# A product by a chosen matrix plus the input: two rows of a sample on each partition, and products in 64x64 tiles

## The chip, the core and the metric

The kernel runs on one core of a Trainium2 chip. The core has engines that run side by side and meet only through semaphores: TensorE (PE) multiplies matrices, VectorE (DVE) works on elements, ScalarE (ACT) only issues loads here, GpSimd (POOL) passes on semaphores and copies a little, and SyncE (SP) issues stores. Sixteen DMA engines move data between the memory of the chip and SBUF, the working memory with 128 partitions. Products land in PSUM, a second memory of 128 partitions.

The metric is the device time in microseconds. The kernel before takes 323.05 us, the median of 3 runs (322.87 to 323.2).

## The reference

```python
# x: (128, 128, 1024) float32; itok_B_0_7: (128,) int32, 0 to 7
# L0_cond_weights: (8, 128, 128) float32
w = weights[subjects]                       # one 128x128 matrix for each sample
out = jnp.einsum('bct,bcd->bdt', x, w)
return x + out
```

For each of 128 samples b, the output is x[b] plus the product of the transposed matrix of its subject with x[b]. A sample has 128 rows (c) of 1024 numbers (t), half a megabyte. 67.1 MB go in, as many come out, and the eight matrices are half a megabyte together.

## The kernel before

A sample lies in SBUF with one row c on each partition: 128 partitions of 1024 numbers. Four samples make a slot of 2 MB, and SBUF holds 12 slots (`x_all`, `SLOTS`). The program runs over 32 turns (`NT`) of four samples, in two halves of two samples (`H`, `G`).

- ScalarE issues 128 loads of one sample each (`load`, line 134), in order. From the thirteenth turn on it waits until the stores of the slot's previous turn have finished (`s_slot`).
- GpSimd waits for the loads of each turn and tells TensorE (`s_ready`).
- TensorE runs a loop of 32 turns (line 268). `multiply` (line 168) waits for the matrices (`s_go`) and for the input (`s_ready`), and makes four products for a half: two samples, and for each the two 512-wide halves of t. A product has the 128x128 matrix of its sample as the stationary operand and streams 512 columns. Its result takes one PSUM bank; the two halves of a turn use one half of PSUM each (`ps[0]`, `ps[1]`).
- VectorE runs a loop of 32 turns (line 263). `add` (line 183) waits for the products of a half, adds PSUM to the input in SBUF (128 x 2048 elements) and writes the sum over the input, in the same slot. `place` (line 163) then copies the two matrices of the next turn's half out of `w_all` into `w0` to `w3`, since the subject of a sample is known only at run time.
- SyncE waits for adds (`s_added`) and issues a store of 2 MB for each of the first 20 turns (`store`, line 142); in the middle of the program it lags four more turns behind the adds (`BEHIND`). The last 12 turns go out in six stores of 4 MB (`PAIR`).

Before the loops the matrices are brought in: one load of 512 KB with 4 KB on each partition, two transposes on VectorE (lines 208 and 227) and 16 copies (line 230, four of them on GpSimd) put row c of every matrix on partition c. Meanwhile TensorE runs three products of zeros (line 200, `IDLE`).

On the DRAM side a load is described as 32 pieces of 16 KB (`ROWS` = 4 rows each), and on the SBUF side as 128 pieces of 4 KB. A store reads 16 KB from each partition and writes it as four rows of 4 KB to four samples.

Of the kernel before, what the change touches and what calls it, by code (L numbers as in the profile page):

```python
# [25 lines left out]
F32 = mybir.dt.float32  # L26
I32 = mybir.dt.int32
ALU = mybir.AluOpType


G = 2
H = 2

N = 512

SLOTS = 12

P_SLOTS = 2

BEHIND = 4  # L40

EARLY = 8
LAST = 8

PAIR = 2
WHOLE = 6

DMA = 16

SORTED = 18  # L50

IDLE = 3

ROWS = 4

# [25 lines left out]
def kernel(  # L81
# [7 lines left out]
    nc = tc.nc  # L89
    B, C, T = x.shape  # L90
    S, _, D = weights.shape
    NT = B // (G * H)

    def sbuf(name, *shape, dtype=F32):
        return ctx.enter_context(nc.sbuf_tensor(name, list(shape), dtype)).ap()


    room = -(nc.sbuf_base + -nc.sbuf_base % 32) % ALIGN
    if room:
        sbuf("room", C, room // 4)  # L100
    x_all = sbuf("x_all", C, SLOTS * H * G * T)
    xs = [
        x_all[:, i * H * G * T : (i + 1) * H * G * T].rearrange("c (q t) -> c q t", t=T)
        for i in range(SLOTS)
    ]
    w_all = sbuf("w_all", C, S, D)
    w_raw, w_mid, w_late = (xs[SLOTS - 1][:, q, :] for q in range(3))
    ws = [sbuf(f"w{i}", C, 1, D) for i in range(H * G)]
    zeros = sbuf("zeros", C, N)
    given, near, wrap = (sbuf(name, 1, B, dtype=I32) for name in ("given", "near", "wrap"))  # L110
    index = sbuf("index", 1, B + H * G, dtype=I32)
    ps = [
        ctx.enter_context(nc.psum_tensor(f"ps{i}", [D, G, T], F32)).ap() for i in range(P_SLOTS)
    ]
# [4 lines left out]
    s_zeros = tc.alloc_semaphore("s_zeros")  # L119
    s_product = tc.alloc_semaphore("s_product")  # L120
# [5 lines left out]
    s_slot = [tc.alloc_semaphore(f"s_slot{k}") for k in range(SLOTS)]  # L126
    s_head = tc.alloc_semaphore("s_head")
    s_sort = tc.alloc_semaphore("s_sort")

    def emptied(i):  # L130
        turns = i // SLOTS
        return DMA * (H * G + 1) * turns - (DMA * G if i >= SLOTS and i % SLOTS == 0 else 0)

    def load(engine, i, q):
        transfer(
            nc,
            engine,
            xs[i % SLOTS][:, q, :],
            x[i * H * G + q].rearrange("(a r) t -> a (r t)", r=ROWS),
        ).then_inc(s_head if i * H * G + q < G else s_slot[i % SLOTS], DMA)  # L140

    def store(i, n):
        at = i % SLOTS * H * G * T
        return transfer(
            nc,
            nc.sync,
            out[i * H * G : (i + n) * H * G].rearrange("g d t -> d g t"),
            x_all[:, at : at + n * H * G * T].rearrange(
                "d (o t) -> d o t", o=1 if i >= NT - WHOLE else n
            ),  # L150
        )

    def subjects_of(i):
        _, subject = nc.values_load_multi_w_load_instructions(
            index[0:1, i] if isinstance(i, slice) else index[0:1, bass.ds(i * (H * G), H * G)],
            engines=[mybir.EngineType.DVE],
            min_val=0,
            max_val=S - 1,
            skip_runtime_bounds_check_because="the index is clamped on the chip above",
        )  # L160
        return subject

    def place(h, subject):
        for q in range(h * G, (h + 1) * G):
            copy = nc.vector.tensor_copy(ws[q], w_all[:, bass.ds(subject[q], 1), :])  # L165
        copy.then_inc(s_go, 1)

    def multiply(slot, h):
        nc.tensor.wait_ge(s_go, 1).then_inc(s_go, -1)
        nc.tensor.wait_ge(s_ready, 1).then_inc(s_ready, -1)  # L170
        for q in range(h * G, (h + 1) * G):
            for t in range(0, T, N):
                at = slot * (H * G * T) + (q * T + t)
                mm = nc.tensor.matmul(  # L174
                    ps[h][:, q % G, t : t + N],
                    ws[q][:, 0, :],
                    x_all[:, bass.ds(at, N)],
                    start=True,
                    stop=True,
                )  # L180
        mm.then_inc(s_product, 1)

    def add(slot, h):
        mine = x_all[:, bass.ds(slot * (H * G * T) + h * G * T, G * T)]
        nc.vector.wait_ge(s_product, 1).then_inc(s_product, -1)  # L185
        nc.vector.tensor_tensor(  # L186
            mine, ps[h].rearrange("d g t -> d (g t)"), mine, ALU.add
        ).then_inc(s_added, 1)

    with tc.tile_critical():  # L190

        nc.sync.dma_start(
            w_raw, weights.rearrange("s (u j) d -> (s u) (j d)", j=S)
        ).then_inc(s_wall, DMA)
        nc.sync.dma_start(given, subjects.rearrange("(o b) -> o b", o=1)).then_inc(s_given, DMA)

        nc.vector.memset(zeros, 0.0).then_inc(s_zeros, 1)  # L197
        nc.tensor.wait_ge(s_zeros, 1)
        for _ in range(IDLE):
            nc.tensor.matmul(  # L200
                ps[P_SLOTS - 1][:, G - 1, :N], zeros[:, :D], zeros, start=True, stop=True
            )

        nc.vector.wait_ge(s_wall, DMA)
        nc.vector.transpose(  # L208
            w_mid.rearrange("p (e h w j) -> p j h e w", e=S, h=4, w=4), w_raw
        ).then_inc(s_sort, 1)  # L210
        nc.vector.memset(index[:, B:], 0).then_inc(s_index, 1)  # L211
        nc.vector.wait_ge(s_given, DMA)
        nc.vector.tensor_scalar(near, given, -S, S - 1, ALU.max, ALU.min).then_inc(s_index, 1)  # L213
# [3 lines left out]
        nc.vector.tensor_tensor(index[:, :B], near, wrap, ALU.add).then_inc(s_index, 1)  # L217
        for i in range(NT):
            if i == SLOTS - 1:
                nc.scalar.wait_ge(s_sort, SORTED)  # L220
            if i >= SLOTS:
                nc.scalar.wait_ge(s_slot[i % SLOTS], emptied(i))
            for q in range(H * G):
                load(nc.scalar, i, q)

        nc.vector.wait_ge(s_sort, 1)
        nc.vector.transpose(w_late, w_mid).then_inc(s_sort, 1)  # L227

        def sort(engine, o, v):
            engine.tensor_copy(  # L230
                w_all[32 * v : 32 * (v + 1), 2 * o : 2 * (o + 1), :],
                w_late[32 * o : 32 * (o + 1)].rearrange("c (e v d) -> c v e d", v=4, d=D)[:, v],
            ).then_inc(s_sort, 1)

        nc.vector.wait_ge(s_sort, 2)
        nc.gpsimd.wait_ge(s_sort, 2)
        for o in range(4):
            for v in range(4):
                sort(nc.gpsimd if v == 3 else nc.vector, o, v)
        for i in range(NT):  # L240
            if i == 0:
                nc.gpsimd.wait_ge(s_head, DMA * G).then_inc(s_ready, 1)
                nc.gpsimd.wait_ge(s_slot[0], DMA * G).then_inc(s_ready, 1)
            else:
                nc.gpsimd.wait_ge(s_slot[i % SLOTS], emptied(i) + DMA * H * G).then_inc(s_ready, H)

        for i in [*range(NT - SLOTS), *range(NT - SLOTS, NT, PAIR)]:
            n = 1 if i < NT - SLOTS else PAIR
            nc.sync.wait_ge(s_added, (i + n + (BEHIND if EARLY <= i < NT - LAST else 0)) * H)
            if i == 0:  # L250
                nc.sync.dma_start(
                    out[: H * G].rearrange("g d t -> d g t"), xs[0]
                ).then_inc(s_slot[0], DMA)
            elif i + n < NT:
                store(i, n).then_inc(s_slot[i % SLOTS], DMA)


        nc.vector.wait_ge(s_index, 4)
        nc.vector.wait_ge(s_sort, SORTED)
        subject = subjects_of(slice(0, H * G))  # L260
        for h in range(H):
            place(h, subject)
        with nc.vector.Fori(0, NT) as turn:  # L263
            subject = subjects_of(turn + 1)
            for h in range(H):
                add(turn % SLOTS, h)
                place(h, subject)
        with nc.tensor.Fori(0, NT) as turn:
            for h in range(H):
                multiply(turn % SLOTS, h)  # L270

    with tc.tile_critical() as waits:
        for i in range(NT - SLOTS, NT - PAIR, PAIR):
            nc.scalar.wait_ge(s_slot[i % SLOTS], emptied(i + SLOTS))
    last = store(NT - PAIR, PAIR)

    tc.add_manual_dep(
        last.ins,
# [31 lines left out]
```

## Time and profile before

| | |
|---|---|
| median of 3 runs | 323.05 us |
| span of the profiled execution, first to last instruction | 320.9 us |
| TensorE busy | 248.9 us (78%), 518 records, mean granted clock 0.893 |
| VectorE busy | 172.6 us (54%) |
| DMA | 134.76 MB, 420 GB/s over the span |
| loads of x | 128 of 512 KB |
| stores | 20 of 2048 KB and 6 of 4096 KB |
| first product of a sample | 14.54 us |
| last add ends | 295.1 us |

How to read the rows: a group of instructions is given with line, engine, operation, output and inputs, the count behind the x, then busy time in us and mean ns of one, then the idle time just before them and what ended it. PE is the matmul records, PEld the weight loads. The rows of busy tenths and GB/s cut the span into 40 slices of 8 us; a 9 is a slice that is 90% busy or more. PEclk is the clock that TensorE was granted, in tenths of full speed. A row of a timeline has the start and the length in us first. A row of windows has the stretch, its length, then the busy time and number of records of PE, PEld, DVE and POOL, then the granted clock, the DMA share and GB/s.

### The profile page before, as it was taken

What the parts mean: (1) busy time and instruction counts of PE and PEld (TensorE: products, weight loads), DVE (VectorE), ACT (ScalarE), POOL (GpSimd) and SP (SyncE); (2) the same over time, 40 slices, a digit from 0 to 9 for tenths busy, and PEclk for the clock granted to TensorE, in tenths of its full rate; (3) what the DMA queues carried; (4) which work ended last, traced back from release to release, by engine and by line L of the source; (5) the groups of instructions that cost most, each with busy time, mean ns of one, the idle gap of its engine ahead of it and who ended that gap; (6) DMA issues with size and microseconds to landing.
All of it is one profiled execution on the core that took longest, in us unless ns stands there. A gap on an engine that the chain in (4) does not pass through costs nothing. (4 is left out here: it accounts for less than half of the span.)

```text
span 320.9 us, 2386 instructions
## 1 busy us (share of the span) xinstructions
PE 248.9 (78%) x518; PEld 102.8 (32%) x518; DVE 172.6 (54%) x216; POOL 1.9 (1%) x8
## 2 busy tenths in 40 slices
PE   6199999999997699998498469988599957874000
PEld 2134444444433244443133224333244422331000
DVE  4636776777676167775435362675367745066000
POOL 0200000000000000000000000000000000000000
PEclk9679999999999599999789797999799989599555
DMA  7999999999999999999999999999999999999996
GB/s 294 425 425 412 426 423 432 429 423 425 425 425 425 425 424 425 425 429 425 429 435 431 427 427 429 425 425 425 425 425 425 425 425 425 427 427 455 429 445 274
DMA packets 10803, 134.76 MB, mean 420 GB/s; under 512 B 2481, under 2 KB 2482, under 8 KB 3122
## 3 DMA queue, kind: packets, MB, share of 16 engines
q1 hardware_dynamic: 4658, 67.64, 49.7%
q10 hardware_dynamic: 6144, 67.12, 49.6%
q14 instruction: 1, 0.01, 0.0%
HBM read 67.63 MB, written 67.11 MB: 420 GB/s over the span
## 5 line engine op out<-in xcount | busy, mean ns | idle before, releaser
L174 PE MATMUL ps<-x_all,w 128*128 x512 | 243.8, 635 | 42.0 <-PEq L170 34.3
L186 DVE TENSOR_TENSOR x_all<-ps,x_all 128x2048 f32 x64 | 146.7, 2292 | 117.3 <-DVEq L185 117.3
L174 PEld LDWEIGHTS ps<-x_all,w 128*128 128x128 f32 x512 | 100.9, 203 | 185.2 <-issue 184.6
L165 DVE COPY w<-w_all 128x128 f32 x132 | 23.2, 219 | 0.8 <-DVE w_all L230 0.8
L200 PE MATMUL ps<-zeros 128*128 128x512 f32 x6 | 5.2, 1033 | 1.7 <-DVE zeros L197 1.7
L230 DVE COPY w_all<-x_all 32x256 f32<-32x256 f32 x12 | 3.9, 326 | 0.4
L208 DVE STREAM_TRANSPOSE x_all<-x_all 128x1024 f32<-128x1024 f32 x1 | 2.0, 1992 | 3.1 <-DMA x_all<-in_L_cond_weights_dram 3.1
L200 PEld LDWEIGHTS ps<-zeros 128*128 128x128 f32 x6 | 1.8, 328 | 3.7 <-issue 2.1
L230 POOL COPY w_all<-x_all 32x256 f32<-32x256 f32 x4 | 1.7, 425 | 8.3 <-DVE x_all L227 8.1
L227 DVE STREAM_TRANSPOSE x_all<-x_all 128x1024 f32<-128x1024 f32 x1 | 1.2, 1225 | 0.0
L197 DVE MEMSET zeros<- 128x512 f32 x1 | 0.5, 485 | 1.0 <-SPq L190 1.0
L217 DVE CUSTOM_DVE_ANT_0 index<-near,wrap 1x256 uint16<-1x256 uint16 x1 | 0.3, 280 | 0.0
L215 DVE TENSOR_SCALAR wrap<-near 1x128 int32<-1x128 int32 x1 | 0.2, 215 | 0.0
L213 DVE TENSOR_SCALAR near<-given 1x128 int32<-1x128 int32 x1 | 0.2, 205 | 0.0
L297 POOL MEMSET const-bfloat16-1.0<- 128x1 bf16 x1 | 0.1, 100 | 0.0
L297 POOL MEMSET const-float32-0.0<- 128x1 f32 x1 | 0.1, 98 | 0.2 <-issue 0.2
L297 POOL MEMSET const-uint8-127<- 128x1 uint8 x1 | 0.1, 98 | 0.0
L297 POOL MEMSET const-float32-1.0<- 128x1 f32 x1 | 0.1, 97 | 0.0
L297 DVE BASE_LOAD x1 | 0.0, 21 | 0.1
L211 DVE MEMSET index<- 1x4 int32 x1 | 0.1, 62 | 0.0
## 6 DMA issues: line engine op xcount, KB each, us to landing
x_all<-in_x_dram ACTq DMA_DIRECT2D x128, 512.0 KB, 34.2
out_dram<-x_all SPq DMA_DIRECT2D x20, 2048.0 KB, 18.3
out_dram<-x_all SPq DMA_DIRECT2D x6, 4096.0 KB, 30.3
x_all<-in_L_cond_weights_dram SPq DMA_DIRECT2D x1, 512.0 KB, 3.7
given<-in_itok_B_dram SPq DMA_DIRECT2D x1, 0.5 KB
```

What stands on the lines that cost most here:

```text
L165: copy = nc.vector.tensor_copy(ws[q], w_all[:, bass.ds(subject[q], 1), :])
L174: mm = nc.tensor.matmul(ps[h][:, q % G, t : t + N], ws[q][:, 0, :], x_all[:, bass.ds(at, N)], start=True, stop=True,)
L186: nc.vector.tensor_tensor(mine, ps[h].rearrange("d g t -> d (g t)"), mine, ALU.add).then_inc(s_added, 1)
L197: nc.vector.memset(zeros, 0.0).then_inc(s_zeros, 1)
L200: nc.tensor.matmul(ps[P_SLOTS - 1][:, G - 1, :N], zeros[:, :D], zeros, start=True, stop=True)
L208: nc.vector.transpose(w_mid.rearrange("p (e h w j) -> p j h e w", e=S, h=4, w=4), w_raw).then_inc(s_sort, 1)
L213: nc.vector.tensor_scalar(near, given, -S, S - 1, ALU.max, ALU.min).then_inc(s_index, 1)
L215: nc.vector.tensor_scalar(wrap, near, 0, S, ALU.is_lt, ALU.mult).then_inc(s_index, 1)
L217: nc.vector.tensor_tensor(index[:, :B], near, wrap, ALU.add).then_inc(s_index, 1)
L227: nc.vector.transpose(w_late, w_mid).then_inc(s_sort, 1)
L230: engine.tensor_copy(w_all[32 * v : 32 * (v + 1), 2 * o : 2 * (o + 1), :], w_late[32 * o : 32 * (o + 1)].rearrange("c (e v d) -> c v e d", ...
L297: nc = _bacc.Bacc("TRN2", target_bir_lowering=False, num_devices=1)
```

## The change

A sample now lies on 64 partitions with two neighbouring rows (`R` = 2) on each, 2048 numbers. Two samples (`H`) fill the 128 partitions, one in the lower half and one in the upper, and two such pairs (`P`) make a turn. Inputs have 8 places of one pair each, 1 MB (`x_in`, `IN`), and sums have 8 slots of one turn each, 2 MB (`x_out`, `OUT`). So a sum is no longer written over its input: an input place is free when its add has run, and a slot of sums is free when its store has finished (`s_out`, which GpSimd passes on to VectorE as `s_room`).

A row of the sample is c = 2a + r with a the partition and r the row on it, and likewise for the output row d = 2a + e. The product is therefore split into four 64x64 products: for each output row e, the sum over r = 0 and 1, accumulated in PSUM. `multiply` makes for each pair of samples 4 pieces (e, half of t) x 2 (r) x 2 (sample h) = 16 products. The innermost loop goes over the two samples, whose pieces are shifted by two so that they write to different banks. The loop of TensorE now covers eight pairs with fixed addresses and runs 8 times.

The matrices come with the rows of both parities on one partition (64 partitions, 8 subjects, pieces of 1 KB), and three copies (two on VectorE, one on GpSimd, `SHARE`) put the columns into the order (r, e, a) for the lower and the upper half of the partitions. There are no transposes. `place` copies a 64x256 matrix for each sample. Five products of zeros run at the start instead of three.

Loads are 64 of 1 MB (8 KB on each partition). Stores stay 20 of 2 MB and 6 of 4 MB, and each reads 16 or 32 KB from a partition and writes it in rows of 8 KB.

```diff
-G = 2
 H = 2
+P = 2
+R = 2
-SLOTS = 12
+IN = 8
+OUT = 8
-BEHIND = 4
+BEHIND = 3
-WHOLE = 6
+WHOLE = 12
-IDLE = 3
+IDLE = 5
+SHARE = 6
...
+    def load(j):
+        at = j % IN * SIZE
         transfer(
             nc,
-            engine,
-            xs[i % SLOTS][:, q, :],
-            x[i * H * G + q].rearrange("(a r) t -> a (r t)", r=ROWS),
+            nc.scalar,
+            x_in[:, at : at + SIZE],
+            x[j * H : (j + 1) * H].rearrange("h (b r) t -> (h b) (r t)", r=ROWS),
...
-            out[i * H * G : (i + n) * H * G].rearrange("g d t -> d g t"),
-            x_all[:, at : at + n * H * G * T].rearrange(
-                "d (o t) -> d o t", o=1 if i >= NT - WHOLE else n
-            ),
+            out[i * Q : (i + n) * Q].rearrange("(p h) (a r) t -> (h a) p (r t)", h=H, r=R),
+            x_out[:, at : at + n * P * SIZE].rearrange("d (o f) -> d o f", o=1),
...
-    def place(h, subject):
-        for q in range(h * G, (h + 1) * G):
-            copy = nc.vector.tensor_copy(ws[q], w_all[:, bass.ds(subject[q], 1), :])
+    def place(p, subject):
+        for h in range(H):
+            copy = nc.vector.tensor_copy(
+                ws[p][h * A : (h + 1) * A],
+                w_all[h * A : (h + 1) * A, bass.ds(subject[p * H + h], 1), :],
+            )
         copy.then_inc(s_go, 1)
-    def multiply(slot, h):
+    def multiply(k):
+        p = k % P
         nc.tensor.wait_ge(s_go, 1).then_inc(s_go, -1)
         nc.tensor.wait_ge(s_ready, 1).then_inc(s_ready, -1)
-        for q in range(h * G, (h + 1) * G):
-            for t in range(0, T, N):
-                at = slot * (H * G * T) + (q * T + t)
-                mm = nc.tensor.matmul(
-                    ps[h][:, q % G, t : t + N],
-                    ws[q][:, 0, :],
-                    x_all[:, bass.ds(at, N)],
-                    start=True,
-                    stop=True,
-                )
+        pieces = [(e, t) for e in range(R) for t in range(0, T, N)]
+        for b in range(len(pieces)):
+            for r in range(R):
+                for h in range(H):
+                    e, t = pieces[(b + 2 * h) % len(pieces)]
+                    rows = slice(h * A, (h + 1) * A)
+                    at = k * SIZE + r * T + t
+                    mm = nc.tensor.matmul(
+                        ps[p][rows, e, t : t + N],
+                        ws[p][rows, 0, r * D + e * A : r * D + (e + 1) * A],
+                        x_in[rows, at : at + N],
+                        start=r == 0,
+                        stop=r == R - 1,
+                    )
         mm.then_inc(s_product, 1)
...
         nc.vector.tensor_tensor(
-            mine, ps[h].rearrange("d g t -> d (g t)"), mine, ALU.add
+            x_out[:, bass.ds(turn % OUT * (P * SIZE) + p * SIZE, SIZE)],
+            ps[p].rearrange("d r t -> d (r t)"),
+            x_in[:, bass.ds(turn % (IN // P) * (P * SIZE) + p * SIZE, SIZE)],
+            ALU.add,
         ).then_inc(s_added, 1)
+    def sort(engine, h, first, last):
+        engine.tensor_copy(
+            w_all[h * A : (h + 1) * A, first:last].rearrange("c s (r e a) -> c (s r) e a", r=R, e=R),
+            w_raw[:, first * R * D : last * R * D].rearrange(
+                "c (g a e) -> c g e a", a=D // R, e=R
+            ),
+        ).then_inc(s_sort, 1)
...
+        for j in range(NP):
+            if j >= IN and j % P == 0:
+                nc.scalar.wait_ge(s_added, j - IN + P)
+            load(j)
...
+        sort(nc.vector, 0, 0, S)
+        sort(nc.vector, 1, SHARE, S)
+        nc.gpsimd.wait_ge(s_wall, DMA)
+        sort(nc.gpsimd, 1, 0, SHARE)
...
         with nc.vector.Fori(0, NT) as turn:
             subject = subjects_of(turn + 1)
-            for h in range(H):
-                add(turn % SLOTS, h)
-                place(h, subject)
-        with nc.tensor.Fori(0, NT) as turn:
-            for h in range(H):
-                multiply(turn % SLOTS, h)
+            nc.vector.wait_ge(s_room, 1).then_inc(s_room, -1)
+            for p in range(P):
+                add(turn, p)
+                place(p, subject)
+        with nc.tensor.Fori(0, NP // IN):
+            for k in range(IN):
+                multiply(k)
```

The order of the instructions on TensorE, from the products of zeros into the loop, before (ISA rows set an address, `ps0` is the first half of PSUM, `w0` the matrix of a sample):

```order
L200 MATMUL ps1<-zeros 128x512 [waits s_zeros]
L200 MATMUL ps1<-zeros 128x512 x2
L192 UNCONDITIONAL_BRANCH
L268 UNCONDITIONAL_BRANCH
L174 ISA [waits s_go,s_ready]
L174 MATMUL ps0<-x_all,w0 128x512
```

and now, where `w0` holds the matrices of both samples of a pair, one in each half of the partitions:

```order
L223 MATMUL ps1<-zeros 128x512 [waits s_zeros]
L223 MATMUL ps1<-zeros 128x512 x4
L214 UNCONDITIONAL_BRANCH
L272 UNCONDITIONAL_BRANCH
L186 MATMUL ps0<-x_in,w0 64x512 [waits s_go,s_ready]
L186 MATMUL ps0<-x_in,w0 64x512 x15
L186 MATMUL ps1<-x_in,w1 64x512 [waits s_go,s_ready]
L186 MATMUL ps1<-x_in,w1 64x512 x15
```

Two more products of zeros stand ahead of the loop, and 16 products of 64 rows stand between two waits where 4 of 128 rows with an address each stood.

On VectorE, from the landing of the matrices to the first index registers, before (`near`, `wrap` and `index` are the subjects, brought into range):

```order
L208 STREAM_TRANSPOSE x_all<-x_all 128x8x4x8x4 [waits s_wall]
L211 MEMSET index 1x4
L213 TENSOR_SCALAR near<-given 1x128 [waits s_given]
L215 TENSOR_SCALAR wrap<-near 1x128 [waits s_index]
L217 ISA index<-near,wrap 1x256 [waits s_index]
L227 STREAM_TRANSPOSE x_all<-x_all 128x1024 [waits s_sort]
L230 COPY w_all<-x_all 32x256 [waits s_sort]
L230 COPY w_all<-x_all 32x256 x11
L154 TENSOR_LOAD index [waits s_sort,s_index]
```

and now:

```order
L225 MEMSET index 1x4
L205 COPY w_all<-x_out 64x2048 [waits s_wall]
L205 COPY w_all<-x_out 64x512
L238 TENSOR_SCALAR near<-given 1x128 [waits s_given]
L240 TENSOR_SCALAR wrap<-near 1x128 [waits s_index]
L242 ISA index<-near,wrap 1x256 [waits s_index]
L158 TENSOR_LOAD index [waits s_sort,s_index]
```

Two transposes and twelve copies gave way to two longer copies, which now stand ahead of the index steps.

On ScalarE, the loads of x, before:

```order
L67 DMA x_all<-in_x_dram 128x1024 x44
L67 DMA x_all<-in_x_dram 128x1024 [waits s_sort]
L67 DMA x_all<-in_x_dram 128x1024 x3
L67 DMA x_all<-in_x_dram 128x1024 [waits s_slot0]
L67 DMA x_all<-in_x_dram 128x1024 x3
L67 DMA x_all<-in_x_dram 128x1024 [waits s_slot1]
```

and now, from the start of the program:

```order
L311 UNCONDITIONAL_BRANCH [waits barrier_Pool_Activation_PE_DVE_SP_release]
L311 UNCONDITIONAL_BRANCH [waits SP_sequencer_49]
L70 DMA x_in<-in_x_dram 128x2048 x8
L70 DMA x_in<-in_x_dram 128x2048 [waits s_added]
L70 DMA x_in<-in_x_dram 128x2048
```

The first wait for room stood after 48 loads of half a megabyte, and it stands now after 8 of one megabyte; it is a wait for adds and no longer for stores.

More of the change, by code (lines that the diff above doesn't have):

```diff
@@ L100 @@
         sbuf("room", C, room // 4)
[L101 to L108, printed above, removed]
-    zeros = sbuf("zeros", C, N)
[L110 to L114, printed above, removed]
+    x_in = sbuf("x_in", C, IN * SIZE)
+    x_out = sbuf("x_out", C, OUT * P * SIZE)
+    w_all = sbuf("w_all", C, S, R * D)
+    w_raw = x_out[:A, (OUT * P - 1) * SIZE :]
+    zeros = sbuf("zeros", C, N)
+    index = sbuf("index", 1, B + Q, dtype=I32)
+    ps = [ctx.enter_context(nc.psum_tensor(f"ps{p}", [C, R, T], F32)).ap() for p in range(P)]
     s_given = tc.alloc_semaphore("s_given")
@@ L217 @@
         nc.vector.tensor_tensor(index[:, :B], near, wrap, ALU.add).then_inc(s_index, 1)
+        nc.gpsimd.wait_ge(s_zeros, 1).then_inc(s_room, OUT)
         for i in range(NT):
[L219 to L240, printed above, removed]
+            if i - OUT in stored:
+                n = 1 if i - OUT < NT - WHOLE else PAIR
+                nc.gpsimd.wait_ge(s_out[i % OUT], stored[i - OUT]).then_inc(s_room, n)
@@ L241 @@
             if i == 0:
-                nc.gpsimd.wait_ge(s_head, DMA * G).then_inc(s_ready, 1)
-                nc.gpsimd.wait_ge(s_slot[0], DMA * G).then_inc(s_ready, 1)
-            else:
[L245 to L255, printed above, removed]
+                nc.gpsimd.wait_ge(s_head, DMA).then_inc(s_ready, 1)
@@ L272 @@
+        with nc.tensor.Fori(0, NP // IN):
+            for k in range(IN):
+                multiply(k)
     with tc.tile_critical() as waits:
[L273 to L275 removed]
+        for i, n in stores[:-1]:
+            if i >= NT - OUT:
+                nc.scalar.wait_ge(s_out[i % OUT], stored[i])
+    last = store(*stores[-1])
     tc.add_manual_dep(
```

63 lines of the change are left out of this document (37 added, 26 removed).

## The prediction

> **What bounds the kernel now.** I read the page's head first, then the table of DMA queues, then the groups of instructions.
>
> ```profile
> span 320.9 us, 2386 instructions
> ...
> PE 248.9 (78%) x518; PEld 102.8 (32%) x518; DVE 172.6 (54%) x216; POOL 1.9 (1%) x8
> ...
> PE   6199999999997699998498469988599957874000
> ...
> PEclk9679999999999599999789797999799989599555
> DMA  7999999999999999999999999999999999999996
> GB/s 294 425 425 412 426 423 432 429 423 425 425 425 425 425 424 425 425 429 425 429 435 431 427 427 429 425 425 425 425 425 425 425 425 425 427 427 455 429 445 274
> DMA packets 10803, 134.76 MB, mean 420 GB/s; under 512 B 2481, under 2 KB 2482, under 8 KB 3122
> ...
> q1 hardware_dynamic: 4658, 67.64, 49.7%
> q10 hardware_dynamic: 6144, 67.12, 49.6%
> ```
>
> The two queues together fill 49.7 + 49.6 = 99.3% of the sixteen DMA engines' span, and nearly every slice moves about 425 GB/s: 134.76 MB at 425 GB/s is 317.1 us of the 320.9. The transfers bound this kernel, and no idle time is left there to win. The span is 2.15 us short of the median of the three runs (323.05); I sum against the span and add those 2.15 us.
>
> TensorE is the second resource, and it is not far behind.
>
> ```profile
> L174 PE MATMUL ps<-x_all,w 128*128 x512 | 243.8, 635 | 42.0 <-PEq L170 34.3
> L186 DVE TENSOR_TENSOR x_all<-ps,x_all 128x2048 f32 x64 | 146.7, 2292 | 117.3 <-DVEq L185 117.3
> L174 PEld LDWEIGHTS ps<-x_all,w 128*128 128x128 f32 x512 | 100.9, 203 | 185.2 <-issue 184.6
> L165 DVE COPY w<-w_all 128x128 f32 x132 | 23.2, 219 | 0.8 <-DVE w_all L230 0.8
> ...
> L230 DVE COPY w_all<-x_all 32x256 f32<-32x256 f32 x12 | 3.9, 326 | 0.4
> ...
> L230 POOL COPY w_all<-x_all 32x256 f32<-32x256 f32 x4 | 1.7, 425 | 8.3 <-DVE x_all L227 8.1
> ```
>
> The code writes 256 products (128 samples, two halves of T), and the profile has 512 matmul records: each float32 product is two records, each with its own weight load. Their mean of 635 ns is no pace, because records overlap. The pace is read from the starts of the weight loads, one for each record, and from the adds:
>
> ```profile
> 2.68 0.34 PEld L200 LDWEIGHTS ps<-zeros 128*128 128x128 f32 x1 [0.52 <-issue]
> 3.53 0.34 PEld L200 LDWEIGHTS ps<-zeros 128*128 128x128 f32 x1 [0.52 <-issue]
> ...
> 60.15 0.19 PEld L174 LDWEIGHTS ps<-x_all,w 128*128 128x128 f32 x1 [0.24 <-issue]
> 60.58 0.19 PEld L174 LDWEIGHTS ps<-x_all,w 128*128 128x128 f32 x1 [0.24 <-issue]
> ```
>
> ```profile
> 59.94 2.29 DVE L186 TENSOR_TENSOR x_all<-ps,x_all 128x2048 f32 x1 [0.81 <-DVEq L185]
> ...
> 67.00 2.29 DVE L186 TENSOR_TENSOR x_all<-ps,x_all 128x2048 f32 x1 [0.81 <-DVEq L185]
> ```
>
> ```profile
> 31.00:100.00 69.00, 68.59 (x157) 28.77 (x156) 49.22 (x58) 0.00 (x0) 1.00 1.01 425
> ```
>
> A record takes 0.43 us at the full clock (60.15 to 60.58) and 0.85 us at the slow one (2.68 to 3.53). From 31 to 100 us TensorE never rests and the granted clock is 1.00. There four samples, which are 16 records, take 67.00 - 59.94 = 7.06 us: 16 x 0.429 = 6.86, and 0.2 for two hand-overs, or 0.1 for each pair of samples. In and out, four samples are 4.19 MB, which takes 9.87 us at 425 GB/s. So TensorE has 2.8 us in hand out of every 9.87. All 512 records at this pace are 220 us, and doubled they are 440 us: this margin does not survive a doubling.
>
> **The change, part by part.**
>
> *Products.* A sample is now 64 partitions with two rows in each, so it needs four 64x64 products (two row parities in, two out) for each half of T where one 128x128 product stood. For a pair of samples that is 16 products instead of 4, each still streaming 512 columns; with two records each that is 32 records for a pair, and 2048 in all. No row of before shows a product of 64x64. The bounds from the nearest row are these. A 64x64 product holds a quarter of the array; if four were always under way, a record would cost 0.429 / 4 = 0.107 us, and 2048 would cost 220 us as now. If each has the array to itself, a record costs 0.429 us and 2048 cost 879 us. I take the middle value, two at a time, 0.215 us for a record, because of the code: the innermost loop alternates between the two samples of a pair, one reading partitions 0 to 63 and writing 0 to 63, the other reading and writing 64 to 127. Those share neither rows nor columns. But all 8 products of one sample read the same half and write the same half, so they follow one another, and half of the array stays empty. That gives 1024 steps of 0.429 us = 439.3 us, and with 64 hand-overs of 0.1 us 445.7 us.
>
> [...]
>
> *Start.* Rows of before:
>
> ```profile
> 0.96 0.41 SPq L192 DMA_DIRECT2D x_all<-in_L_cond_weights_dram  x1
> ...
> 1.43 0.32 SPq L195 DMA_DIRECT2D given<-in_itok_B_dram  x1
> ```
>
> ```profile
> 1.67 5.16 PE L200 MATMUL ps<-zeros 128*128 128x512 f32 x6 [1.67 <-DVE zeros L197]
> 14.54 2.07 PE L174 MATMUL ps<-x_all,w 128*128 x2 [7.71 <-DVE w L165]
> ```
>
> ```profile
> 4.71 1.99 DVE L208 STREAM_TRANSPOSE x_all<-x_all 128x1024 f32<-128x1024 f32 x1 [3.10 <-DMA x_all<-in_L_cond_weights_dram]
> 6.56 0.20 DVE L213 TENSOR_SCALAR near<-given 1x128 int32<-1x128 int32 x1
> ...
> 13.63 0.63 DVE L165 COPY w<-w_all 128x128 f32 x4 [0.85 <-DVE w_all L230]
> ...
> 292.81 2.29 DVE L186 TENSOR_TENSOR x_all<-ps,x_all 128x2048 f32 x1 [0.81 <-DVEq L185]
> 295.02 0.35 DVE L165 COPY w<-w_all 128x128 f32 x2
> ```
>
> Two transposes and 16 copies become three copies. The matrices land at 4.71 us as now; they now come in 1 KB pieces, which no row shows, so 0 to +2 us, of which I take 0 since it is the same half megabyte at an empty machine. VectorE's two copies have 2048 and 512 elements per partition. Two rows of before give its price: from 128 elements (219 ns) to 256 (326 ns) it is 0.84 ns each, and the add's 2048 in 2292 ns is 1.12 ns, so I take 1 ns each and about 60 ns for each copy, 2.7 us. POOL's 1536 elements at 425 / 256 = 1.66 ns are 2.55 us beside it. The four small index steps take about 0.8 us (the first, of 0.20, stands above), the index registers 0.85 us (the idle before 13.63), and placing 64x256 matrices about 0.9 us up to the first product. That is 4.71 + 2.7 + 0.8 + 0.85 + 0.9 = 10.0 us for the first product, against 14.54 now. Ten filler records instead of six keep TensorE busy to 8 or 10 us, so I take the full clock from the start; if it starts slow as before, some 5 us more.
>
> *Steady state.* VectorE does for each pair one add of 2.29 us and two copies of 64x256 of about 0.33 us each, 3 us against the 6.96 us that the products now take, and it works on one half of PSUM while TensorE fills the other: hidden. Loads need an add to free an input place; eight places are 8.4 MB, about 20 us of transfers, and the transfers need 4.9 us for a pair where TensorE needs 6.96, so inputs are always there and the input places are always full. Sums have places of their own: a store frees one every 13.9 us and lasts a third of that. Nothing but TensorE is late.
>
> *Tail.* Today the last add ends at 295.1 us and the stores that queue behind it fill the rest of the 320.9. Bound by TensorE there is no such queue, and the last store is bare: its 4.19 MB take 9.87 us at 425 GB/s, and the start and the landing of a transfer that finds the engines free come on top.
>
> ```profile
> out_dram<-x_all SPq DMA_DIRECT2D x6, 4096.0 KB, 30.3
> x_all<-in_L_cond_weights_dram SPq DMA_DIRECT2D x1, 512.0 KB, 3.7
> ```
>
> The 512 KB of the matrices take 3.7 us to landing, of which 1.2 are data at 425 GB/s, so that share is 2.5 us (the 30.3 us of a 4 MB store are its wait in the full queues). With the last add (2.29) and 1 us to close the program: 15.7 us.
>
> *Pieces.* Of the packets of now, 3122 - 2482 = 640 are of 2 to 8 KB, and the other 7681 average (134.76 - 2.6) / 7681 = 17.2 KB. Twice longer pieces on the other side of a transfer could move the 425 GB/s either way, by an amount that no row shows; while TensorE is the bound this is worth nothing but a tenth of a microsecond in the last store.
>
> Sum: 10.0 + 445.7 + 15.7 = 471.4 us of span, and with 2.15 us **473 us**, 46% over the 323.05.
>
> **Rivals.**
>
> *The transfers stay the bound (faster).* If 64x64 records cost less than I take, by more being under way at once or by a shorter stream, the point of decision is the transfers' 4.93 us for a pair: (4.93 - 0.1) / 32 = 0.151 us for a record. My bounds (0.107 to 0.429) contain it; against it is the program order, in which no third tile is used. Then the 317 us of transfers rule, TensorE hides again, and only pieces, start and tail count: the slices of 294 and 274 GB/s at the two ends have some 5 us in them, and 1% of pace is 3.2 us. I give 321.5 us with 318 to 325 around it.
>
> *Weight loads no longer hide.* Today a load of 0.19 us lies inside every 0.43 us step (60.15, 60.58). The count of loads goes to 2048, two for each step. If one of them stops the stream, a step is 0.429 + 0.19 = 0.62 us: 1024 x 0.62 + 6.4 + 25.7 + 2.15 = 669 us. [...] The trace of before disagrees for full-size loads, which use the same 128 rows and hide all the same.
>
> *One at a time, or the slow clock.* If records run one by one, 2048 x 0.429 = 879 us and 34 around it: 913 us. If they pair but the clock is granted at half, as in the rows at 2.68 and 3.53 us, 1024 x 0.853 = 873 us, much the same. For it: nothing in the trace shows two records on the array at once. Against it: the two samples share neither rows nor columns.
>
> **Chances.** Pairs at full clock: 0.50, with a range of its own of 460 to 510 us (at most one lost step of 0.43 us for each of the 64 hand-overs is 27 us; a slow start 5 us). The transfers stay the bound: 0.26. Loads exposed: 0.10. One at a time or half clock: 0.12. Something else: 0.02. The likeliest and the transfer-bound case together hold 0.76, so the range also takes in the exposed loads and ends at 680; it begins at 318. A measurement here tells changes of over 0.2% (0.65 us) from none. Within the transfer-bound case I put 0.14 on faster, 0.04 on within 0.2% and 0.08 on slower; with all other cases slower by far: 0.14, 0.04 and 0.82.
>
> **What the profile after would show.** Right: the DMA row falls from 9 to 6 or 7 in every slice and the mean to about 290 GB/s; PE is 9 from 10 us to the end with a granted clock near 1; adds come every 7 us; VectorE waits for products and not the loads; the first product starts near 10 us. Wrong: adds every 5 us with DMA at 9 (transfers still rule), adds every 10 us (loads exposed) or every 14 us (one by one, or a granted clock of 0.5). The forecast falls if a 64x64 record, taken from the starts of weight loads, costs anything but about 0.215 us.

## The result and the profile after

The changed kernel takes 486.86 us (486.74 to 487.14, 4 runs) against 323.12 us: a ratio of 1.507 (1.505 to 1.509). The forecast was 473 us. The head of the page after, its rows of slices, its three main groups and two of its DMA issues:

```profile
span 485.0 us, 5137 instructions
...
PE 449.2 (93%) x2058; PEld 158.4 (33%) x2058; DVE 182.8 (38%) x204; POOL 2.8 (1%) x5
...
PE   6079999999999999999999999999999999999960
...
PEclk9579999999999999999999999999999999999995
DMA  8911888877888344678888888888883976999408
GB/s 307 385 43 23 335 335 315 295 288 286 293 309 312 151 173 173 232 289 289 311 301 312 341 313 299 285 299 284 309 308 151 357 335 238 439 426 430 197 1 347
...
L186 PE MATMUL ps<-x_in,w 64*64 64x512 f32 x2048 | 441.9, 591 | 17.7 <-PEq L178 17.7
L186 PEld LDWEIGHTS ps<-x_in,w 64*64 64x64 f32 x2048 | 155.5, 134 | 304.0 <-issue 304.0
L197 DVE TENSOR_TENSOR x_out<-ps,x_in 128x2048 f32 x64 | 146.6, 2291 | 266.2 <-DVEq L196 266.2
...
x_in<-in_x_dram ACTq DMA_DIRECT2D x64, 1024.0 KB, 8.2
...
x_out<-in_L_cond_weights_dram SPq DMA_DIRECT2D x1, 512.0 KB, 20.4
```

The bound has moved. TensorE is 90% busy or more in every slice from the fourth to the third from the end, with a granted clock of nine tenths or more. The DMA engines, busy in every slice before, now mostly stand at 7 or 8 tenths and move about 300 GB/s. VectorE's idle time ahead of the adds grew from 117 to 266 us: it waits for products. There are 2048 records, as worked out. The matrices take 20.4 us to land, where they took 3.7.

The pace of the products is read from the weight loads in the middle of the program, and the ends of the run from VectorE's and TensorE's timelines:

```profile
100.19 0.15 PEld L186 LDWEIGHTS ps<-x_in,w 64*64 64x64 f32 x2 [0.28 <-issue]
100.62 0.15 PEld L186 LDWEIGHTS ps<-x_in,w 64*64 64x64 f32 x2 [0.28 <-issue]
```

```profile
26.71 441.89 PE L186 MATMUL ps<-x_in,w 64*64 64x512 f32 x2048 [17.70 <-PEq L178]
```

```profile
21.36 2.89 DVE L205 COPY w_all<-x_out 64x2048 f32<-64x2048 f32 x2 [19.75 <-DMA x_out<-in_L_cond_weights_dram]
...
25.82 1.21 DVE L169 COPY w<-w_all 64x256 f32 x4 [0.76 <-DVE index L242]
...
468.88 2.29 DVE L197 TENSOR_TENSOR x_out<-ps,x_in 128x2048 f32 x1 [3.90 <-DVEq L196]
```

Two weight loads, and so two records, start in every step of 0.43 us: 0.215 us for a record. The products run without a break from 26.71 us for 441.89 us. What follows them to the end of the span is 485.0 - 468.6 = 16.4 us.

### The profile page after: what moved, and what is told of

It reads as the page before. It is cut to its first block, busy times and chain, and to the rows that moved or that the text cites. A ratio compares the mean times of both kernels' runs of the same rounds, so it can differ in the third digit from the quotient of the medians.

```text
span 485.0 us, 5137 instructions
## 1 busy us (share of the span) xinstructions
PE 449.2 (93%) x2058; PEld 158.4 (33%) x2058; DVE 182.8 (38%) x204; POOL 2.8 (1%) x5
## 5 line engine op out<-in xcount | busy, mean ns | idle before, releaser
L186 PE MATMUL ps<-x_in,w 64*64 64x512 f32 x2048 | 441.9, 591 | 17.7 <-PEq L178 17.7
L186 PEld LDWEIGHTS ps<-x_in,w 64*64 64x64 f32 x2048 | 155.5, 134 | 304.0 <-issue 304.0
L197 DVE TENSOR_TENSOR x_out<-ps,x_in 128x2048 f32 x64 | 146.6, 2291 | 266.2 <-DVEq L196 266.2
L169 DVE COPY w<-w_all 64x256 f32 x132 | 37.4, 283 | 1.7 <-DVE index L242 0.8
L205 DVE COPY w_all<-x_out 64x2048 f32<-64x2048 f32 (+1 forms) x2 | 2.9, 1430 | 19.8 <-DMA x_out<-in_L_cond_weights_dram 19.7
L223 PE MATMUL ps<-zeros 128*128 128x512 f32 x10 | 7.3, 907 | 1.7 <-DVE zeros L220 1.7
L223 PEld LDWEIGHTS ps<-zeros 128*128 128x128 f32 x10 | 2.9, 302 | 5.3 <-issue 3.6
L205 POOL COPY w_all<-x_out 64x1536 f32<-64x1536 f32 x1 | 2.6, 2573 | 20.9 <-DMA x_out<-in_L_cond_weights_dram 20.9
## 6 DMA issues: line engine op xcount, KB each, us to landing
x_out<-in_L_cond_weights_dram SPq DMA_DIRECT2D x1, 512.0 KB, 20.4
```

Of the source, the lines that this page charges most:

```text
L169: copy = nc.vector.tensor_copy(ws[p][h * A : (h + 1) * A], w_all[h * A : (h + 1) * A, bass.ds(subject[p * H + h], 1), :],)
L186: mm = nc.tensor.matmul(ps[p][rows, e, t : t + N], ws[p][rows, 0, r * D + e * A : r * D + (e + 1) * A], x_in[rows, at : at + N], start=r == 0,
L197: nc.vector.tensor_tensor(x_out[:, bass.ds(turn % OUT * (P * SIZE) + p * SIZE, SIZE)], ps[p].rearrange("d r t -> d (r t)"), x_in[:, bass.d ...
L205: engine.tensor_copy(w_all[h * A : (h + 1) * A, first:last].rearrange("c s (r e a) -> c (s r) e a", r=R, e=R), w_raw[:, first * R * D : la ...
L223: nc.tensor.matmul(ps[P - 1][:, R - 1, :N], zeros[:, :D], zeros, start=True, stop=True)
```

## The experiments

Two questions were open. Does a 64x64 record cost 0.215 us because two are under way, or because it is shorter by itself? And why did the first product come at 26.7 us and not at 10?

**One sample of a pair alone.** The upper sample's products are left out, and the products of zeros at the start, eight instead of five, write to all banks of PSUM.

```diff
-                for h in range(H):
+                for h in range(1):
...
-        for _ in range(IDLE):
...
+        for p, e, t in [(p, e, t) for p in range(P) for e in range(R) for t in range(0, T, N)]:
...
```

> The products of the upper sample of every pair are left out (the results of the upper 64 partitions are the input alone), and the products of zeros at the start go to all eight banks. Theory, two at a time: a 64x64 record costs 0.43 us by itself and only shares this time with the record of the other half, so the lower sample's chain alone is still 1024 x 0.43 = 440 us and the time stays at 487 us, with the granted clock near 1 or, should half the work count as too little, at half and then far over 487. Rival, a smaller product simply streams faster: a record costs 0.215 us by itself, the chain halves to 220 us, the transfers bound and the time falls to about 330 to 340 us.

Measured: 919.27 us (one run). The weight loads in the middle, and the window from 300 to 890 us:

```profile
100.42 0.23 PEld L186 LDWEIGHTS ps<-x_in,w 64*64 64x64 f32 x1 [0.63 <-issue]
101.27 0.23 PEld L186 LDWEIGHTS ps<-x_in,w 64*64 64x64 f32 x1 [0.63 <-issue]
```

```profile
300.00:890.00 590.00, 590.00 (x693) 157.12 (x692) 121.46 (x130) 0.00 (x0) 0.50 0.38 146
```

One record for each step of 0.85 us, the step that a 128x128 record has at the slow clock in the kernel before (2.68 to 3.53 us), and a granted clock of 0.50 although TensorE has no idle time in those 590 us. Half the records took longer than all of them. A lone 64x64 record therefore takes as long as a 128x128 one, here 0.85 us at half clock for both; the shorter stream falls. The half clock is a second effect, which the expectation had left room for.

**The two samples one after the other.** All products stay; only the loop order changes.

```diff
-        for b in range(len(pieces)):
-            for r in range(R):
-                for h in range(H):
+        for h in range(H):
+            for b in range(len(pieces)):
+                for r in range(R):
```

> All 16 products of a pair stay, but the loop over the two samples is the outermost: eight products of the lower half, then eight of the upper. Theory, two at a time by program order: neighbours in the program now share their half and follow one another, 2048 x 0.43 = 879 us of products, and with 26.7 us ahead and 18 us behind about 924 us. Rival, TensorE looks far enough ahead to pair them in any order, or a record costs 0.215 us by itself: 487 us.

Measured: 720.08 us (one run), between the two theories. VectorE's adds, the weight loads between them, and a window:

```profile
98.17 2.29 DVE L197 TENSOR_TENSOR x_out<-ps,x_in 128x2048 f32 x1 [7.45 <-DVEq L196]
...
118.99 2.29 DVE L197 TENSOR_TENSOR x_out<-ps,x_in 128x2048 f32 x1 [7.45 <-DVEq L196]
```

```profile
100.35 0.13 PEld L186 LDWEIGHTS ps<-x_in,w 64*64 64x64 f32 x1 [0.30 <-issue]
100.78 0.13 PEld L186 LDWEIGHTS ps<-x_in,w 64*64 64x64 f32 x1 [0.30 <-issue]
101.21 0.19 PEld L186 LDWEIGHTS ps<-x_in,w 64*64 64x64 f32 x3 [0.30 <-issue]
101.64 0.19 PEld L186 LDWEIGHTS ps<-x_in,w 64*64 64x64 f32 x2 [0.24 <-issue]
102.07 0.19 PEld L186 LDWEIGHTS ps<-x_in,w 64*64 64x64 f32 x2 [0.24 <-issue]
102.55 0.13 PEld L186 LDWEIGHTS ps<-x_in,w 64*64 64x64 f32 x1 [0.30 <-issue]
...
106.42 0.19 PEld L186 LDWEIGHTS ps<-x_in,w 64*64 64x64 f32 x3 [0.29 <-issue]
```

```profile
60.00:700.00 640.00, 640.00 (x1969) 217.28 (x1966) 169.28 (x183) 0.00 (x0) 1.00 0.50 190
```

Two pairs take 20.82 us, 24.3 steps of 0.429 us for a pair, between 16 (always two) and 32 (always one). Most steps have one record. The steps in which two or three loads start come as a group of three, and the next group begins 5.21 us later (101.21 and 106.42), 12 steps of 0.43 us for 16 records, as many as one half of a pair has. If in strict program order only the last record of one half and the first of the next shared a step, twice for a pair, it would be 30 steps, an estimate; 24.3 were measured. So the order of the program counts (487 us with the samples in turn, 720 here), but not strictly. The rows do not tell the two halves apart, so which records share a step, and how they come to, is not shown. The single steps at a granted clock of 1.00 also give what the first experiment could not, the cost of a lone 64x64 record at full clock: 0.43 us, the same as of a 128x128 one. This part is settled: two at a time, each at full length.

**The same PSUM bank.** The pieces of the two samples are no longer shifted.

```diff
-                    e, t = pieces[(b + 2 * h) % len(pieces)]
+                    e, t = pieces[b]
```

> The two samples' pieces are not shifted any more, so the two products under way at once write to the lower and the upper partitions of the same PSUM bank. Theory of the prediction, rows and columns alone decide: 487 us as it is. Rival, two products cannot use one bank at once: they follow one another, about 924 us, or something between.

Measured: 487.18 us (one run), and two weight loads start in each step of 0.43 us as before. The shift does nothing here: two records that write to different halves of the partitions of one bank run together all the same, and the time is that of the changed kernel (486.86 us).

**All four quarters of the array.** The same products, with the odd output rows written to the other half of PSUM.

```diff
+        for t in range(0, T, N):
+            for r in range(R):
+                for o in range(R):
+                    for h in range(H):
+                        e = o
...
+                        half = h if o == 0 else 1 - h
...
-                        ps[p][rows, e, t : t + N],
+                            ps[p][half * A : (half + 1) * A, e, t : t + N],
...
+        for h in range(H):
+            rows = slice(h * A, (h + 1) * A)
+            other = slice((1 - h) * A, (2 - h) * A)
+            last = nc.vector.tensor_tensor(
+                x_out[rows, bass.ds(a + T, T)], ps[p][other, 1, :], x_in[rows, bass.ds(b + T, T)], ALU.add
+            )
```

> Nothing is left out. The same 16 products of a pair are spread over all four quarters of the array: odd output rows go to the other half of PSUM, so that each sample uses two quarters, and the add of 128 x 2048 becomes one of 128 x 1024 and two of 64 x 1024 that cross the halves (about 3.7 us for a pair instead of 2.3). Theory, the empty half of the array made the changed kernel slow: with four records under way the products need 220 us again, and the time is that of the kernel with half of the products, about 359 us. Rival, the two records of a product block the program order, so that never more than two are under way whatever the quarters: 487 us. If three run on average, the transfers hide it and the time is 359 as well.

Measured: 357.58 us, 1.107 (1.105 to 1.109) times the kernel before. Weight loads and a window:

```profile
70.44 0.18 PEld L187 LDWEIGHTS ps<-x_in,w 64*64 64x64 f32 x4 [0.25 <-issue]
70.87 0.18 PEld L187 LDWEIGHTS ps<-x_in,w 64*64 64x64 f32 x4 [0.25 <-issue]
```

```profile
60.00:120.00 60.00, 49.86 (x440) 18.28 (x444) 58.26 (x68) 0.00 (x0) 1.00 1.01 430
```

Four loads in each step of 0.43 us, so four records at once. TensorE has idle time again, and the transfers are back at 430 GB/s. The empty half of the array was most of what made the changed kernel slow: 129 of the 164 us that it lost come back, and the time is that of the kernel with half of the products below (359 us), as expected.

**The kernel before, with every product made twice.**

```diff
-            for t in range(0, T, N):
+            for t in [t for t in range(0, T, N) for _ in range(2)]:
```

> The kernel before, with every product made twice, so that TensorE has 1024 steps of 0.43 us as in the changed kernel; nothing else is touched. Theory, the doubled steps alone made the changed kernel slow: 14.5 us to the first product, 1024 x 0.429 + 6.4 = 446 us, 2.8 us for the slow clock at the start, 16 us after the last product and 2 us outside the span, about 481 us, near the 487 of the change. Rival, the layout, its buffers and its pieces cost much of the change by themselves: 460 us or less.

Measured: 474.12 us, a ratio of 1.468 (1.466 to 1.471). TensorE's timeline:

```profile
14.55 441.15 PE L174 MATMUL ps<-x_all,w 128*128 x1024 [7.40 <-DVE w L165]
```

The expected 481 us was 7 us too long, most of it the 6.4 us of hand-overs, which this kernel does not pay. Doubled steps alone, in the old layout, give 441.15 us of products against 441.89 in the changed kernel. Its first product comes 12.2 us earlier, and its time is 12.7 us shorter. So the steps and the later start are nearly the whole difference; beyond the start, the layout, its buffers and its pieces cost about 1 us while TensorE is the bound.

**Matrices first.** One wait ahead of ScalarE's first load.

```diff
+        nc.scalar.wait_ge(s_wall, DMA)
         for j in range(NP):
```

> ScalarE waits for the landing of the matrices before it issues the first load of x. Theory, the 1 KB packets of the matrices take turns with 16 KB packets of x on every DMA engine (32 x (0.616 + 0.046) = 21 us): with the engines to themselves the matrices land at 4 to 5 us, the first product comes at about 10.5 us and the time falls by 16 to 471 us. Rival, a load in 1 KB pieces is slow by itself (20 us for 512 of them): the matrices land at 20 us all the same, the loads of x come after, and the time rises to about 490 us.

Measured: 470.28 us (469.25 to 471.36), a ratio of 1.455 (1.451 to 1.458). First the DMA queues of the changed kernel in its first 22 us, then VectorE and TensorE of this one:

```profile
q10 hardware_dynamic: 528, 7.08, 85.2%
q1 hardware_dynamic: 530, 0.52, 6.9%
```

```profile
6.37 2.90 DVE L205 COPY w_all<-x_out 64x2048 f32<-64x2048 f32 x2 [4.76 <-DMA x_out<-in_L_cond_weights_dram]
```

```profile
11.73 441.38 PE L186 MATMUL ps<-x_in,w 64*64 64x512 f32 x2048 [3.45 <-PEq L178]
```

In the changed kernel the queue of the matrices (q1) passed 0.52 MB, 512 pieces of 1 KB, while that of x (q10) passed 7.08 MB, some 430 pieces of 16 KB; the rest of the 530 and 528 packets are nearly all under 512 B. About as many small pieces as large ones went through, 512 and some 430, as if they took turns; the order of the pieces is not shown. Without x beside them the matrices are there at 6.37 instead of 21.36 us, the first product comes 15.0 us earlier, and the time falls by 16.6 us. Alone, the 1 KB pieces land 1.7 us later than the 4.71 us of the kernel before; the other 15 us come from the company of x.

**What the transfers would have given.** To ask what the rival "the transfers stay the bound" was worth, half of the products are left out (only even rows are multiplied), first alone and then with the matrices first.

```diff
-            for r in range(R):
+            for r in range(1):
...
-                        stop=r == R - 1,
+                        stop=True,
```

> Half of the products are left out (only the even rows of the input are multiplied), so TensorE has 1024 records for 512 steps of 0.43 us, 220 us; all transfers, adds and copies stay. Theory, TensorE alone made the changed kernel slow, and the new pieces move at the old pace or slightly above it (16 KB packets of 611 ns against 616): 317 us of transfers, and a hole of about 11 us near 20 to 31 us, in which the eight input places are full and no add has run because the matrices came late: about 330 us. Rival, the eight input places or the sums' own slots hold up the transfers as well: 345 us or more.

> As the kernel with half of the products, and ScalarE waits for the matrices before the first load of x. Theory: no hole is left after the start, the transfers start some 3 us later, and the time is 319 to 324 us: what the new layout would give if TensorE kept up. Rival, the buffers hold the transfers up: 335 us or more.

Measured: 359.18 us, a ratio of 1.110 (1.107 to 1.113), and with the matrices first 344.60 us, 1.067 (1.065 to 1.068). Both theories missed, 330 us and 319 to 324 us. The times lie where the rivals had them, which blamed the buffers, and far above the 317 us of transfers. The slices of the second, three adds and two windows near its end:

```profile
GB/s 92 430 397 416 432 430 432 428 432 430 430 430 430 430 297 432 432 432 430 432 430 428 430 430 430 430 432 432 451 407 435 430 437 424 428 399 347 0 186 307
```

```profile
288.55 2.29 DVE L197 TENSOR_TENSOR x_out<-ps,x_in 128x2048 f32 x1 [10.97 <-DVEq L196]
...
305.32 2.29 DVE L197 TENSOR_TENSOR x_out<-ps,x_in 128x2048 f32 x1 [10.73 <-DVEq L196]
...
322.28 2.29 DVE L197 TENSOR_TENSOR x_out<-ps,x_in 128x2048 f32 x1 [10.91 <-DVEq L196]
```

```profile
310.00:325.00 15.00, 9.57 (x32) 3.12 (x32) 4.07 (x6) 0.00 (x0) 0.66 0.28 122
325.00:342.00 17.00, 0.25 (x2) 0.00 (x0) 2.84 (x4) 0.00 (x0) 0.58 0.58 248
```

In the middle most slices read 428 to 432 GB/s, where before they read 425, about 1% more. One slice in the middle drops to 297, and the rest of the loss is at the two ends: the first slice, and the last four. There the adds of the last three turns wait 11 us each, for products whose inputs land late. The last three pairs of loads, issued at 247, 256 and 270 us, take 31, 38 and 41 us to land, where the median of all loads is 24; three stores of 4 MB, issued at 256 and 270 us, share the engines with them. TensorE starts the products of these turns at 282.1, 298.6 and 315.4 us, when GpSimd reports their inputs; the trace shows GpSimd waiting for no slot of sums at that time, so the slots, which the next expectation names, were not what was late. The next kernel, with half of the products too, lets two loads go ahead of the matrices, and stores single turns with the lag kept to turn 28:

```diff
-LAST = 8
+LAST = 4
...
-WHOLE = 12
+WHOLE = 0
...
+            if j == P:
+                nc.scalar.wait_ge(s_wall, DMA)
             load(j)
```

> As the kernel with half of the products, with two edits to the order: the first two loads of x go ahead of the wait for the matrices and the others behind it, and the stores all go out in 2 MB with the lag of three turns kept to turn 28. Theory, the 345 us of the kernel that waited for the matrices held 4 us at the start and some 20 us at the end, in which adds waited for slots of sums that a pair of turns releases only together: both go, and 135 MB at 430 GB/s and about 7 us at the ends give 320 to 324 us. Rival, eight input places are too few near the end, whatever the stores do: 335 to 345 us.

Measured: 332.13 us, a ratio of 1.029 (1.026 to 1.032). Its slices:

```profile
GB/s 246 231 443 224 391 419 441 419 439 429 429 433 425 437 421 417 425 433 429 429 433 427 439 425 433 425 429 429 425 433 425 431 425 435 427 433 402 431 425 245
```

The end is mended: from the sixth slice on none but the last is below 400, and the last turn's products start at 301.3 us instead of 315.4. Whether single stores or the longer lag did it was not separated. The start is not: the first five slices average 307 GB/s, and 41 us x (1 - 307/430) is 12 us. The theory of 320 to 324 us missed by 8 to 12 us, about what the start lost, and the rival of 335 to 345 us, which saw the cause near the end, missed too.

**Nothing left out, everything mended.** Four quarters, with this start and end, and then with all loads behind the matrices instead.

> Nothing is left out: the four quarters of the array, and the two edits to the order of the transfers. Theory: both lacks of the changed kernel, the half-empty array and the order of the transfers, are mended, and with a pace of 430 instead of 425 GB/s the time is 320 to 324 us, level with the kernel before or 1% below it. Rival, the shifted adds make VectorE late (4.3 us for a pair against 4.9 of transfers): 330 us or more.

> As the kernel with four quarters and the changed order of transfers (340.4 us), but all loads of x wait for the matrices, as in the kernel that came to 470 us. Theory: two loads ahead held the matrices back to 11 us and the first add to 23 us, when the eight input places were already full, and that cost about 5 us more than a wait of 4 us at the start: 333 to 337 us. Rival, VectorE's 4.38 us for a pair against 4.88 of transfers makes the rest, and the start counts for nothing: 339 to 341 us.

Measured: 340.40 us, 1.053 (1.051 to 1.056), and 335.50 us, 1.042 (1.035 to 1.049). The first misses its 320 to 324 and lies with its rival, a VectorE that comes late (330 us or more); the second gains the expected 5 us from the start. VectorE's busy tenths and the GB/s of the second:

```profile
DVE  2389999999998999999999999768959789859800
GB/s 79 423 429 370 429 435 429 427 433 431 423 437 427 431 289 358 429 431 429 433 431 427 431 433 425 431 435 425 431 433 425 433 431 429 429 431 141 441 423 333
```

In four quarters the adds and copies of a pair take VectorE 4.38 us, where the transfers take 4.88. Away from the two ends the transfers drop twice, to 289 and 358 GB/s at 117 to 133 us and to 141 at 300 to 308 us, and VectorE works without a pause through both: from 300 to 310 us it is busy for 9.64 of 10 us while the DMA engines stand at 45%. In both places the stores wait for adds three turns on (`BEHIND`); the second drop ends when the next stores are issued, at 305.9 us. So there the transfers waited for VectorE's adds, and the three slices hold about 10 us against 430 GB/s. The kernel with half of the products has the same lag and the same end, a pair takes its VectorE about 3 us, and it has no such slice after the sixth. This is read from the traces; no run made VectorE faster with four quarters, or the lag shorter. No version of this layout tried here beats the kernel before.

## Why the prediction was right, and where it was not

- *Products*: right, in the mechanism too. 2048 records, two at a time, 0.215 us each: 445.7 forecast, 441.9 measured. The choice of two at a time had no row behind it, only the program order, and a chance of 0.50; the run with one sample alone (one record in each step) and the one with the samples one after the other (24.3 steps for a pair in place of 16) agree with it. The 0.1 us for each hand-over is not paid, neither here nor in the kernel before with doubled products (441.15 us for 1024 steps); why it is paid in the kernel before was not tried.
- *Start*: the step that failed. "The matrices land at 4.71 us as now" took the load to meet "an empty machine". It met eight loads of x: in the first 22 us its 512 pieces of 1 KB went through beside some 430 of 16 KB, and it landed at 21.4 us. The first product came at 26.7 instead of 10.0, and these 16.7 us are more than the whole miss of 14; that the products came out 3.8 us shorter hid some of it. Of the 16.7 us, 1.7 are the 1 KB pieces by themselves (alone they land at 6.37 us instead of 4.71; the prediction named 0 to 2 us for this and took 0), and 15.0 are the company of x. The copies were priced well: 2.89 us against 2.7, POOL's 2.57 against 2.55.
- *Full clock*: the filler products ended at 9.0 us and the late matrices left a gap of 17.7 us, and the products then start at a granted clock of 0.50 (26.7 to 31 us): the first five steps take 0.85 us each, and from 36 to 460 us the clock reads 1.00. That cost about 2 us, inside the 5 us that the prediction allowed for.
- *Steady state*: right. VectorE waits for products only; loads and stores have time in hand.
- *Tail*: 15.7 forecast, 16.4 measured. Outside the span 2.15 and 1.9.
- *Weight loads exposed*: fell. Two loads of 0.15 us lie in each step of 0.43 us. With the samples one after the other, where neighbouring products in the program read the same 64 partitions, most steps have one load of 0.13 us and take 0.43 us all the same. In these runs a step stays 0.43 us whether the loads in it take 0.13 or 0.19 us (the samples one after the other), 0.15 (the changed kernel), 0.18 (four quarters) or 0.19 (the kernel before).
- *One at a time or the slow clock*: both prices were seen in runs, 0.43 us for a lone record and 0.85 at half clock, but neither applies to the order that the change chose. There two loads start in each step of 0.43 us, and four with all four quarters.
- *The transfers stay the bound, 321.5 us*: it did not come, and its price was too low. With TensorE out of the way this layout gives 359 us as it stands, and 332 at the best start and end tried with half of the products. The pace was judged well (430 instead of 425); the shorter run-ahead at the start and the large stores beside the last loads were overlooked, because with TensorE as the bound they cost nothing.

Terms against the profile:

| | forecast | measured |
|---|---|---|
| to the first product | 10.0 | 26.7 |
| products | 445.7 | 441.9 |
| after them | 15.7 | 16.4 |
| outside the span | 2.15 | 1.9 |
| sum | 473 (the terms give 473.55) | 486.9 |

## What to carry to other kernels

Before a product is cut into smaller tiles, count the steps. Here a 64x64 record took the 0.43 us of a 128x128 one, and four times as many records kept TensorE's time only with four under way at once, in all four quarters: 244.6 us busy with the products, against 441.9 with two under way and 243.8 in the kernel before. Here a small transfer in small pieces that was started beside large ones got about one piece through for each of theirs (512 and some 430), and came 15 us later than alone; what the program waits for at the start goes alone and first. TensorE needed 7.06 of every 9.87 us before, over 70% of the time; a resource so far in use has no room for a doubling, however much another one rules today.

## What the runs showed that was not expected

- With one 64x64 record in each step (one sample of a pair alone) TensorE had no idle time and was granted half the clock for 590 us on end: 0.50, 0.85 us for each record. With two in each step (the changed kernel) it was granted 1.00 from 36 to 460 us, with the samples one after the other (32 records in 24.3 steps) 1.00 from 60 to 700 us, and with one 128x128 record in each step (the kernel before) 1.00 from 31 to 100 us. What decides between the two clocks, no run shows.
- With the samples one after the other a pair took 24.3 steps, where strict program order was estimated at 30; and with four quarters four loads start in each step of 0.43 us, where the rival had never more than two under way.
- Two records that write to one PSUM bank, in different halves of its partitions, did not slow each other here: 487.18 us against 486.86.
